# Distances and residual rows in one group of products, and the first block's edges and next messages ahead of its inverse

## The chip, the cores and the metric

The kernel runs on one core of a Trainium2 chip. The metric is the device time of one execution in microseconds; the kernel before was measured three times, and one more execution was taken by the hardware profiler. Five engines work side by side, each through its own queue in order: TensorE (PE, matrix products; its weight loads are shown as PEld), VectorE (DVE), ScalarE (ACT), GpSimd (POOL) and SyncE (SP, which here only issues DMAs). Products land in PSUM, which has eight banks of 512 float32 per partition; VectorE and ScalarE read them out.

## The reference

Two graph layers on 128 graphs of 128 nodes with 256 features, all in float32. The change lies in layer 0, where h is the rectified layer norm of x:

```python
h  = relu(bn(conv1d(xc, conv1_w)))             # 1 tap
h  = bn(conv1d(h, conv2_w, pad 8))             # 17 taps
x_conv = relu(h + xc)
s  = x @ w_se.T + b_se                         # 3 numbers a node
sq = sum(s * s)
dist = sq[:, :, None] + sq[:, None, :] - 2 * s @ s.T
A    = exp(-dist) * mask
msg  = relu(x @ w_msg.T + b_msg)
x_nmp = A @ msg
gi = concat(x_conv, x_nmp) @ w_ih.T + b_ih ;  gh = x @ w_hh.T + b_hh
r, z = sigmoid(gi_r + gh_r), sigmoid(gi_z + gh_z)
out  = (1 - z) * tanh(gi_n + r * gh_n) + z * x
```

Layer 1 takes the first 25 nodes of each graph, in five groups of nodes, through two normalised graph convolutions and adds the result.

## The kernel before

The graphs are taken in 32 blocks of four (`BB` = 4, `NBLK` = 32). The 17-tap convolution is done in the frequency domain in an earlier part of the kernel; its result lies in DRAM as 128 main rows (`yd`) and 8 residual rows (`yrd`) per graph. The part that the change touches runs from about 449 us to the end and is a loop over blocks: `gates(i)` makes block i's gates while, in between its products, the inputs of block i + 1 are made.

What is made for a block, in functions of these names:

- `messages`: seven products (L544, 130 columns: 128 of the messages and the 3 of s, by a scheme with seven products for eight), evicted by VectorE, ScalarE and GpSimd into `msg`; then VectorE writes s and its squares into the small tile `lr` (L570 to L575).
- `conv_out`, the inverse transform: into four banks, first the residual rows (L519: four products that are 16 rows deep, each on another fourth of the array's rows, left open), then the main rows (L523: two products a bank, which close it). VectorE (L526) and ScalarE (L527) make `xc` of it.
- `edge_terms`: two transposes of `lr` (L582), which ScalarE copies to `lt` (L584).
- `edges`: four products 5 rows deep (L594, the distances; again on different fourths of the array), each in a bank of its own; ScalarE takes the exponential (L597), VectorE multiplies with the mask (L599).
- `x_nmp`: eight products (L609), copied to `xn` by ScalarE (L614) and VectorE (L612).
- `gate_inputs`: sums of blocks of the three inputs (L632 to L635), on GpSimd for `xc` and `ht`, on VectorE for `xn`.

`gates` goes through four units of seven products each, in the order 1, 2, 6, 5, 3, 7, 4 (z: 1, 6, 5, 7, 4, 2, 3). They are r (three matmuls a product: `ht`, `xc`, `xn`), nh (one: `ht`), nn (two: `xc`, `xn`) and z (three). All are L658. Each product takes a bank and is evicted in turn: product 1 by ScalarE (m1, L661), 2 by VectorE (L663), 6 by VectorE (u2, L666), 5 by ScalarE (m5, L669), which lets GpSimd make u4 = u2 + m5 (L671); 3 is added to u4 by VectorE (L673), 7 gives u3 on VectorE (L676), from which GpSimd makes the last quarter (L677), and 4 is subtracted by VectorE (L679). After the r unit, ScalarE applies two sigmoids (L694); after nn, two tanh (L704). The hook of the z unit runs what is left of the next block's inputs.

After each product `step()` is called: every other time it goes on by one `yield` in `beside_gates(i + 1)`, which calls the functions above, and otherwise in layer 1. So the order of the yields in `beside_gates` is the order of the work on TensorE. `beside_gates` also takes block i - 1 through `back` (its output, and the layer-1 preparation, with the transposes L822 and the product L835). Layer 1's own products are L926, L986 and L905; they stand between block 12's and 14's, between 22's and 24's, and at the end. For block 0 there are no gates to work beside: `sums_ahead` is called after each product of block 0's nh unit, which is taken first there, and makes block 0's inputs at fixed places of that unit.

Banks come from one pool of eight (`bank()`). Which bank a product gets, and so which eviction it waits for, is settled when the program is built.

Of the kernel before, what the change touches and what calls it, by code (L numbers as in the profile page):

```python
# [17 lines left out]
BB = 4  # L18
# [8 lines left out]
MW = 130  # L27
# [47 lines left out]
def gnn_kernel(ctx: ExitStack, tc: tile.TileContext, io, out0: bass.AP, out1: bass.AP):  # L75
    nc = tc.nc
    x, adjT = io["x"], io["adjT"]
    NBLK, N, _, D = x.shape
# [288 lines left out]
    v = {}  # L367
# [138 lines left out]

    A_s, xcs, xns, ts, msgs, outs, lrs, xts = ({} for _ in range(8))

    def conv_out(i):

        ht = hts[i]
        ym, yr = loaded.pop(i)
        xc = wk.tile([P, C, T], F32, tag="xc", name="xc", bufs=2)
        pss = [[bank()[:, :H] for _ in range(2)] for _ in range(C)]
        for o in range(C):
            for h, ps in enumerate(pss[o]):
                r0 = 32 * (2 * o + h)
                g = slice(r0, r0 + 2 * NR)
                nc.tensor.matmul(ps, yr[g, :], idr[g, :], start=True, stop=False)  # L519
        for o in range(C):  # L520
            for h, ps in enumerate(pss[o]):
                for b in range(2):
                    nc.tensor.matmul(ps[:, b * N:(b + 1) * N], ym[:, 2 * h + b, o * P:(o + 1) * P], idm,  # L523
                                     start=False, stop=b == 1)
                v = slice(h * H, (h + 1) * H)
                nc.vector.scalar_tensor_tensor(xc[:, o, v], ps, sc2[:, o:o + 1], ht[:, o, v], op0=ALU.mult, op1=ALU.add)  # L526
            nc.scalar.activation(xc[:, o, :], xc[:, o, :], AF.Relu, bias=sh2[:, o:o + 1])  # L527
            yield
        xcs[i] = xc

    def messages(i):


        msg = wk.tile([P, BB, 2, MW], F32, tag="msg", name="msg", bufs=1)
        b11, b12, b21, b22 = quarters(hts[i])
        t1, t2, t3, t4 = (ts[i][2][:, m] for m in range(4))
        s2, s3, s4 = (swm[:, m] for m in range(3))
        ops = ((wms[:, 0, 0], b11), (wms[:, 1, 0], b21), (s4, b22), (wms[:, 1, 1], t4), (wms[:, 0, 1], t1), (s2, t2), (s3, t3))

# [35 lines left out]
        nc.vector.tensor_scalar(lr[:, 0, :, 4:5], lr[:, 1, :, 3:4], -1.0, None, op0=ALU.mult)  # L575
        yield

    def edge_terms(i):

        ps = bank()  # L580
        for k in range(2):
            nc.tensor.transpose(ps[:, k * P:(k + 1) * P], lr[:, k].rearrange("p b r -> p (b r)"), ident)  # L582
        lt = wk.tile([P, 2, P], F32, tag="lt", name="lt", bufs=2)
        nc.scalar.copy(lt.rearrange("p k n -> p (k n)"), ps[:, :2 * P])  # L584
        lrs[i] = lt

    def edges(i):

        at = ats.pop(i)
        lt = lrs.pop(i)  # L590
        pd = [bank() for _ in range(BB)]
        for b in range(BB):
            g = slice(32 * b, 32 * b + 5)
            nc.tensor.matmul(pd[b][:, :N], lt[g, 0, :], lt[g, 1, :], start=True, stop=True)  # L594
        e = wk.tile([P, BB, N], F32, tag="e", name="e", bufs=1)
        for b in range(BB):
            nc.scalar.activation(e[:, b, :], pd[b][:, :N], AF.Exp)  # L597
            if b % 2:
                nc.vector.tensor_mul(e[:, b - 1:b + 1, :], e[:, b - 1:b + 1, :], at[:, b - 1:b + 1, :])  # L599
        A_s[i] = e  # L600

    def x_nmp(i):

# [399 lines left out]
    def beside_gates(i):  # L1003

        ends = back(i - 2, *back_loads(i - 2)) if i > 1 else iter(())
        if i < NBLK:
            parts = messages(i)
            next(parts)
            yield
            next(parts)  # L1010
            next(ends, None)
            yield
            yield
            inverse = conv_out(i) if i else iter(())
            next(inverse, None)
            next(ends, None)
            yield
            edge_terms(i)
            next(ends, None)
            yield  # L1020
            for _ in inverse:
                yield
            edges(i)
            yield
            next(ends, None)
            yield
            yield
            yield from x_nmp(i)
        for _ in ends:
            yield  # L1030
            if i == NBLK:
                yield
# [12 lines left out]
    load_y(0)  # L1045
    load_y(1)
    degs = degrees(*degree_loads())
    begin = beside_gates(0)
    for _ in range(2):
        next(begin)  # L1050
    held = [7]

    def sums_ahead():

        held[0] -= 1
        if held[0] == 3:
            for _ in conv_out(0):
                pass
            gate_inputs(0, (0,))
            while 0 not in lrs:  # L1060
                next(begin)
        if held[0] == 2:
            while 0 not in A_s:
                next(begin)
        if held[0] == 0:
            for _ in begin:
                pass
            gate_inputs(0, (1,))
            gate_inputs(1, (2,))

    layer1s = []
    for i in range(NBLK):
        first = beside_gates(i + 1)
        turn = [0]

        def step():

            next(degs, None)
            turn[0] += 1
            if (turn[0] % 2 if i else turn[0] % 3) and next(first, STOP) is not STOP:  # L1080
                return
            for _ in range(2 if i == NBLK - 1 else 1):
                while layer1s and next(layer1s[0], STOP) is STOP:
                    layer1s.pop(0)

        if i + 2 < NBLK:
            load_h(i + 2)
            load_y(i + 2)
        xts[i] = wk.tile([P, C, T], F32, tag="xt", name="xt", bufs=2)
        nc.sync.dma_start(xts[i], io["xT"][i])  # L1090

        def nxt():
            for _ in first:
                pass
            if i + 1 < NBLK:
                gate_inputs(i + 1, (0, 1))
            if i + 2 < NBLK:
                gate_inputs(i + 2, (2,))

        gates(i, step, nxt, None if i else sums_ahead)  # L1100
        if (i + 2) * BB == PARTS[0]:
            for q in (-5, -4, -3):
                prepare(q)
        for k in range(len(PARTS)):
            if i * BB == first_of[k + 1]:
                layer1s.append(layer1(k))
# [136 lines left out]
```

## Time and profile before

| | |
|---|---|
| median of three executions | 1865.76 us (1865.35 to 1867.79) |
| profiled execution, its own time | 1866.29 us |
| span of the profiled execution | 1864.5 us, mean granted TensorE clock 0.997 |
| TensorE busy | 1843.8 us, 99% of the span |
| VectorE busy | 1361.9 us, 73% |
| ScalarE busy | 737.0 us, 40% |
| GpSimd busy | 652.9 us, 35% |
| distances, L594: 256 records | 16.1 us busy |
| residual rows, L519: 256 records | 24.6 us busy |

The span is the time from the first instruction's start to the last one's end. A float32 product is two records on TensorE, one per pass. Matmuls overlap in the pipeline, so a record (380 ns for 256 columns) is longer than the step from one to the next (216 ns); steps are read from the starts. The idle time behind an engine's row, in square brackets in a timeline, is followed by what ended it. The "granted clock" is the share of its full speed at which TensorE was allowed to run.

### The profile page before, as it was taken

The page shows a single profiled execution, that of the slowest core. Times are in us where ns is not written, and L with a number is a line of the kernel's source. Part 1 is how long each engine was busy: PE and PEld are TensorE (multiplying, and loading weights), DVE is VectorE, ACT ScalarE, POOL GpSimd, SP SyncE. Part 2 cuts the span into 40 slices and gives each one's busy share as a digit, 9 for nine tenths or more (in the row PEclk, how much of TensorE's full clock was granted, in tenths as well). Part 3 has the DMA queues.
Part 4 walks back from the last instruction along what each step waited for, and adds up shares of the span by engine and source line. Part 5 has one row for each costly group of instructions (what it writes and reads, how often), then busy time and mean ns, then how long its engine had stood idle before and what let it go on. Part 6 is the DMA issues. An engine that isn't in the chain of part 4 may idle for free.

```text
span 1864.5 us, 31417 instructions
## 1 busy us (share of the span) xinstructions
PE 1843.8 (99%) x10982; PEld 1592.3 (85%) x10982; DVE 1361.9 (73%) x3312; ACT 737.0 (40%) x1668; POOL 652.9 (35%) x803
## 2 busy tenths in 40 slices
PE   8999999999999999999999999999999999999998
PEld 6888888887888888888888888888888888888887
DVE  6888865555988888888656778888756788888643
ACT  4666651111443334333334433433343343334334
POOL 1111125675343544454321345444412243544200
PEclk9999999999999999999999999999999999999999
DMA  8788778997532233224234422333232433222125
GB/s 294 285 303 334 302 277 285 344 325 244 171 88 75 72 85 94 76 73 124 73 90 119 120 75 72 88 83 113 61 103 85 131 95 87 73 72 70 39 89 158
DMA packets 219420, 267.98 MB, mean 144 GB/s; under 512 B 106210, under 2 KB 182967, under 8 KB 217215
## 3 DMA queue, kind: packets, MB, share of 16 engines
q1 hardware_dynamic: 214079, 248.04, 42.8%
q10 hardware_dynamic: 5184, 17.93, 2.4%
q8 instruction: 88, 1.44, 0.3%
q14 instruction: 69, 0.57, 0.1%
HBM read 169.24 MB, written 96.67 MB: 143 GB/s over the span
## 4 chain that ended last, share of the span: by engine, by line
PE 90%; DVE 4%; DMA 2%; POOL 2%; SPq 1%; issue 1%; ACT 1%; ACTq 0%; DVEq 0%; POOLq 0%
PE bank L658 43%; PE bank L332 6%; PE bank L235 6%; PE bank L926 5%; PE bank L986 5%; PE bank L544 4%; PE bank L251 4%; PE bank L523 3%; PE bank L327 3%; PE bank L609 3%; PE bank L172 2%; PE bank L221 1%; PE bank L905 1%; DMA nt<-in_adjN_dram 1%; PE bank L835 1%; PE bank L519 1%
## 5 line engine op out<-in xcount | busy, mean ns | idle before, releaser
L658 PE MATMUL bank<-t,sw 128*128 128x256 f32 x1152 | 291.4, 380 | 0.0
L671 POOL TENSOR_TENSOR u<-u,m 128x256 f32<-128x256 f32 x128 | 93.7, 732 | 465.1 <-ACT m L669 386.7
L658 PEld LDWEIGHTS bank<-t,sw 128*128 128x128 f32 x1152 | 212.7, 190 | 29.0 <-issue 2.3
L658 PE MATMUL bank<-t,wih 128*128 128x256 f32 x768 | 197.2, 379 | 0.0
L658 PEld LDWEIGHTS bank<-t,wih 128*128 128x128 f32 x768 | 145.5, 190 | 20.9 <-issue 0.9
L235 PE MATMUL bank<-wc,ht 128*128 128x256 f32 x512 | 126.0, 390 | 0.0
L324 POOL TENSOR_TENSOR vs<-v 128x256 f32<-128x256 f32 x134 | 99.0, 763 | 70.9 <-DMA v<-vd 44.1
L658 PE MATMUL bank<-t,whh 128*128 128x256 f32 x384 | 117.5, 388 | 0.0
L567 ACT ACTIVATE msg<-msg 128x512 f32<-128x512 f32 x64 | 36.9, 622 | 196.7 <-DVE msg L563 196.7
L658 PE MATMUL bank<-xc,wih 128*128 128x256 f32 x384 | 114.4, 379 | 0.0
L658 PE MATMUL bank<-xn,wih 128*128 128x256 f32 x384 | 114.2, 379 | 0.0
L986 PE MATMUL bank<-w,hh 128*125 128x256 f32 (+9 forms) x480 | 113.5, 380 | 0.6 <-DVE hh L931 0.6
L658 PE MATMUL bank<-ht,whh 128*128 128x256 f32 x384 | 109.9, 380 | 0.0
L205 POOL TENSOR_TENSOR rs<-ve,mhalf 128x4 f32<-128x4 f32 x32 | 32.3, 1009 | 217.0 <-DVE ve L203 209.9
L926 PE MATMUL bank<-ax,w 128*128 128x500 f32 (+8 forms) x416 | 107.0, 396 | 0.1
L235 PEld LDWEIGHTS bank<-wc,ht 128*128 128x128 f32 x512 | 93.8, 193 | 15.1 <-issue 0.3
L986 PEld LDWEIGHTS bank<-w,hh 128*125 128x125 f32 (+9 forms) x480 | 84.3, 178 | 18.8 <-DVE hh L931 1.0
L180 ACT COPY sp<-bank 128x272 f32<-128x272 f32 x208 | 67.0, 408 | 68.7 <-PE bank L172 52.9
L676 DVE TENSOR_TENSOR u<-bank,u 128x256 f32<-128x256 f32 x128 | 53.7, 420 | 54.6 <-PE bank L658 53.0
L321 DVE SCALAR_TENSOR_TENSOR s<-X 128x256 f32<-128x256 f32 x67 | 45.0, 672 | 64.9 <-PE bank L332 64.9
L669 ACT COPY m<-bank 128x256 f32<-128x256 f32 x128 | 47.3, 369 | 104.5 <-PE bank L658 104.5
L926 PEld LDWEIGHTS bank<-ax,w 128*128 128x128 f32 x416 | 69.9, 190 | 19.4 <-issue 12.3
(206 smaller groups left out, 4415.8 us busy)
## 6 DMA issues: line engine op xcount, KB each, us to landing
vd<-sp SPq DMA_DIRECT2D x16, 2176.0 KB
v<-vd SPq DMA_DIRECT2D x34, 1024.0 KB
w<-in_w_dram SPq DMA_DIRECT2D x40, 512.0 KB
ln<-in_x_dram SPq DMA_DIRECT2D x32, 512.0 KB
htd<-ht SPq DMA_DIRECT2D x32, 512.0 KB
yd<-ys ACTq DMA_DIRECT2D x32, 512.0 KB
ht<-htd SPq DMA_DIRECT2D x32, 512.0 KB
ym<-yd SPq DMA_DIRECT2D x32, 512.0 KB
```

What stands on the lines that cost most here:

```text
L180: nc.scalar.copy(dst, s)
L235: nc.tensor.matmul(pv[:, bb, :], ht[:, c, b * N:(b + 1) * N], wc1[:, c, :], start=c == 0, stop=c == C - 1)
L251: nc.tensor.matmul(ps[:, bb * LW:(bb + 1) * LW], h1[:, 2 * h + bb, c * P:(c + 1) * P], fd, start=True, stop=True)
L324: nc.gpsimd.tensor_tensor(vs[:, c], vr[c], vi[c], op=ALU.add)
L327: nc.tensor.matmul(p1[:, :D], a[:, c], vs[:, c], start=c == 0, stop=c == C - 1)
L332: nc.tensor.matmul(ps[:, k * D:(k + 1) * D], u[:, c], w[c], start=c == 0, stop=c == C - 1)
L523: nc.tensor.matmul(ps[:, b * N:(b + 1) * N], ym[:, 2 * h + b, o * P:(o + 1) * P], idm, start=False, stop=b == 1)
L544: nc.tensor.matmul(ps[:, b, :], d[:, b * N:(b + 1) * N], w, start=True, stop=True)
L658: nc.tensor.matmul(ps, w, d, start=n == 0, stop=n == len(pairs) - 1)
L671: nc.gpsimd.tensor_tensor(got["u4"], got["u2"], got["m5"], op=ALU.add)
L926: nc.tensor.matmul(pv[:, q - q0, :], w1s[k5 + g][:, c, q * P:(q + 1) * P], xv[:, c], start=c == 0, stop=c == C - 1)
L986: nc.tensor.matmul(ps[:n1, :D], hh[:, q, at:at + n1], w2s[k5 + g][:, q, :], start=q == 0, stop=q == HID // P - 1)
```

## The change

From the second block on, the four distances are computed in the same banks as the residual rows, in columns 256 to 383 beside the inverse's columns 0 to 255, and right before them: eight thin products in one group instead of two groups of four. `edges` and `conv_out` are split accordingly into `residual_rows` (distances, residual rows, and by `exponentials` the exponential and the mask) and a `conv_out` that starts with the main rows. In `beside_gates` the transposes of `lr` move ahead to where the inverse began; the group follows two yields later, then the main rows, then x_nmp. The whole has one yield more.

Block 0 keeps its distances apart (`edges`), but the order is changed: transposes and distances first, at other places of the nh unit; then the first four message products of block 1; then residual rows and inverse; then x_nmp. `gate_inputs(1, (2,))`, which those messages need, is called earlier, and the message tile `msg` has two buffers instead of one.

```diff
+    def residual_rows(i):
+
+        yr = loaded[i][1]
+        pss = [[bank() for _ in range(2)] for _ in range(C)]
+        if i:
+            lt = lrs.pop(i)
+            for b in range(BB):
+                g = slice(32 * b, 32 * b + 5)
+                nc.tensor.matmul(pss[b // 2][b % 2][:, H:H + N], lt[g, 0, :], lt[g, 1, :], start=True, stop=True)
         for o in range(C):
             for h, ps in enumerate(pss[o]):
                 r0 = 32 * (2 * o + h)
                 g = slice(r0, r0 + 2 * NR)
-                nc.tensor.matmul(ps, yr[g, :], idr[g, :], start=True, stop=False)
+                nc.tensor.matmul(ps[:, :H], yr[g, :], idr[g, :], start=True, stop=False)
+        if i:
+            exponentials(i, [pss[b // 2][b % 2][:, H:H + N] for b in range(BB)])
+        return pss
...
-        msg = wk.tile([P, BB, 2, MW], F32, tag="msg", name="msg", bufs=1)
+        msg = wk.tile([P, BB, 2, MW], F32, tag="msg", name="msg", bufs=2)
...
-    def edges(i):
+    def exponentials(i, pd):
 
         at = ats.pop(i)
-        lt = lrs.pop(i)
-        pd = [bank() for _ in range(BB)]
-        for b in range(BB):
-            g = slice(32 * b, 32 * b + 5)
-            nc.tensor.matmul(pd[b][:, :N], lt[g, 0, :], lt[g, 1, :], start=True, stop=True)
         e = wk.tile([P, BB, N], F32, tag="e", name="e", bufs=1)
         for b in range(BB):
-            nc.scalar.activation(e[:, b, :], pd[b][:, :N], AF.Exp)
+            nc.scalar.activation(e[:, b, :], pd[b], AF.Exp)
             if b % 2:
                 nc.vector.tensor_mul(e[:, b - 1:b + 1, :], e[:, b - 1:b + 1, :], at[:, b - 1:b + 1, :])
         A_s[i] = e
+
+    def edges(i):
+
+        lt = lrs.pop(i)
+        pd = [bank()[:, :N] for _ in range(BB)]
+        for b in range(BB):
+            g = slice(32 * b, 32 * b + 5)
+            nc.tensor.matmul(pd[b], lt[g, 0, :], lt[g, 1, :], start=True, stop=True)
+        exponentials(i, pd)
...
             yield
-            inverse = conv_out(i) if i else iter(())
-            next(inverse, None)
-            next(ends, None)
-            yield
             edge_terms(i)
             next(ends, None)
             yield
+            yield
+            if i:
+                inverse = conv_out(i, residual_rows(i))
+            else:
+                edges(i)
+                inverse = iter(())
+            yield
+            next(ends, None)
+            yield
             for _ in inverse:
                 yield
-            edges(i)
-            yield
             next(ends, None)
-            yield
             yield
             yield from x_nmp(i)
...
-    begin = beside_gates(0)
+    begin, second = beside_gates(0), beside_gates(1)
     for _ in range(2):
         next(begin)
+    gate_inputs(1, (2,))
     held = [7]
 
     def sums_ahead():
 
         held[0] -= 1
         if held[0] == 3:
-            for _ in conv_out(0):
-                pass
-            gate_inputs(0, (0,))
             while 0 not in lrs:
                 next(begin)
-        if held[0] == 2:
+        if held[0] == 1:
             while 0 not in A_s:
                 next(begin)
         if held[0] == 0:
+            next(second)
+            for _ in conv_out(0, residual_rows(0)):
+                pass
+            gate_inputs(0, (0,))
             for _ in begin:
                 pass
             gate_inputs(0, (1,))
-            gate_inputs(1, (2,))
...
-        first = beside_gates(i + 1)
+        first = beside_gates(i + 1) if i else second
```

More of the change, by code (lines that the diff above doesn't have):

```diff
@@ L507, in gnn_kernel @@
     A_s, xcs, xns, ts, msgs, outs, lrs, xts = ({} for _ in range(8))
[L509 to L514, printed above, removed]
+    def residual_rows(i):
[6 more added lines that the diff above has]
+                nc.tensor.matmul(pss[b // 2][b % 2][:, H:H + N], lt[g, 0, :], lt[g, 1, :], start=True, stop=True)
         for o in range(C):
@@ L518, in conv_out @@
                 g = slice(r0, r0 + 2 * NR)
-                nc.tensor.matmul(ps, yr[g, :], idr[g, :], start=True, stop=False)
+                nc.tensor.matmul(ps[:, :H], yr[g, :], idr[g, :], start=True, stop=False)
+        if i:
+            exponentials(i, [pss[b // 2][b % 2][:, H:H + N] for b in range(BB)])
+        return pss
+    def conv_out(i, pss):
+        ht = hts[i]
+        ym = loaded.pop(i)[0]
+        xc = wk.tile([P, C, T], F32, tag="xc", name="xc", bufs=2)
         for o in range(C):
@@ L525, in conv_out @@
                 v = slice(h * H, (h + 1) * H)
-                nc.vector.scalar_tensor_tensor(xc[:, o, v], ps, sc2[:, o:o + 1], ht[:, o, v], op0=ALU.mult, op1=ALU.add)
+                nc.vector.scalar_tensor_tensor(xc[:, o, v], ps[:, :H], sc2[:, o:o + 1], ht[:, o, v], op0=ALU.mult, op1=ALU.add)
             nc.scalar.activation(xc[:, o, :], xc[:, o, :], AF.Relu, bias=sh2[:, o:o + 1])
@@ L1013, in beside_gates @@
             yield
-            inverse = conv_out(i) if i else iter(())
-            next(inverse, None)
+            edge_terms(i)
             next(ends, None)
             yield
-            edge_terms(i)
+            yield
[5 more added lines that the diff above has]
+            yield
             next(ends, None)
```

## The prediction

> **What bounds the kernel now.** I read the page first (busy time by engine), then TensorE's waits, then the timelines of the engines through one ordinary block. The page:
>
> ```profile
> PE 1843.8 (99%) x10982; PEld 1592.3 (85%) x10982; DVE 1361.9 (73%) x3312; ACT 737.0 (40%) x1668; POOL 652.9 (35%) x803
> ```
>
> TensorE (PE) is busy for all but 20.7 us of the 1864.5 us span. A change can gain only by taking work from TensorE, or a few us of waits; it can lose wherever it makes TensorE wait. The two waits near this change:
>
> ```profile
> PE bank L519 <- DMA yr<-yrd: 3.2, 1, 3.2
> PE bank L609 <- DVE e L599: 0.4, 2, 0.2
> ```
>
> Both are in block 0. Now block 5, TensorE's timeline (start, length, line, operands, count of records; a 128x256 product is two records, 0.433 us):
>
> ```profile
> 622.06 1.03 PE L658 MATMUL bank<-t,wih 128*128 128x256 f32 x4
> 623.02 0.71 PE L519 MATMUL bank<-idr,yr 16*128 16x256 f32 x8
> 623.66 1.16 PE L523 MATMUL bank<-idm,ym 128*128 128x128 f32 x8
> 624.66 1.03 PE L658 MATMUL bank<-ht,whh 128*128 128x256 f32 x4
> 625.52 0.38 PE L582 MATMUL bank<-ident,lr 128*128 128x128 f32 x2
> 625.74 0.38 PE L822 MATMUL bank<-ident,xl 128*100 128x128 f32 x2
> ...
> 626.82 1.05 PE L523 MATMUL bank<-idm,ym 128*128 128x128 f32 x8
> 627.72 0.60 PE L658 MATMUL bank<-ht,sw 128*128 128x256 f32 x2
> 628.15 0.59 PE L658 MATMUL bank<-t,sw 128*128 128x256 f32 x2
> 628.67 0.50 PE L594 MATMUL bank<-lt 5*128 5x128 f32 x8
> 629.11 0.70 PE L658 MATMUL bank<-t,whh 128*128 128x256 f32 x2
> 629.64 0.59 PE L658 MATMUL bank<-xc,wih 128*128 128x256 f32 x2
> ```
>
> Each thin group (16 or 5 rows deep, four products side by side in the array) has a way in, a body and a way out. Residual rows, L519: the products before end at 622.06 + 4 x 0.2165 = 622.93 and the group starts at 623.02 (in: 0.09); body 0.64 to 623.66; the eight records after it take 1.00, where the same eight at 626.82 take 0.90 (out: 0.10). Distances, L594: 628.15 + 0.43 = 628.58, start 628.67 (0.09); body 0.44; the next product takes 0.53 for 0.43 (0.10). So 0.83 and 0.63 us.
>
> The other engines at the same time; first ScalarE, then VectorE and GpSimd:
>
> ```profile
> 622.71 0.35 ACT L669 COPY m<-bank 128x256 f32<-128x256 f32 x1
> 624.36 0.72 ACT L694 ACTIVATE o<-o,brz 128x512 f32<-128x512 f32 x1 [1.29 <-DVE o L673]
> 625.50 0.72 ACT L694 ACTIVATE o<-o,brz 128x512 f32<-128x512 f32 x1 [0.43 <-POOL o L677]
> 626.13 0.35 ACT L661 COPY m<-bank 128x256 f32<-128x256 f32 x1
> 626.39 0.72 ACT L527 ACTIVATE xc<-xc,bn 128x512 f32<-128x512 f32 x1
> 627.01 0.36 ACT L584 COPY lt<-bank 128x256 f32<-128x256 f32 x1
> ```
>
> ```profile
> 622.61 0.17 DVE L575 TENSOR_SCALAR lr<-lr 128x4 f32<-128x4 f32 x1
> 626.52 0.42 DVE L663 TENSOR_TENSOR nh<-bank,m 128x256 f32<-128x256 f32 x1 [0.55 <-ACT m L661]
> 627.20 0.41 DVE L666 TENSOR_TENSOR u<-bank,m 128x256 f32<-128x256 f32 x1
> ```
>
> ```profile
> 623.14 0.72 POOL L671 TENSOR_TENSOR u<-u,m 128x256 f32<-128x256 f32 x1 [3.18 <-ACT m L669]
> ```
>
> What to see: the evictions run far behind TensorE. `lr` is complete at 622.78, and nh's first copy (L661) runs at 626.13, behind the second sigmoid. TensorE doesn't wait, because its banks are free in time.
>
> **The change, ordinary block.** 26 blocks have this pattern (2 to 12, 15 to 22, 25 to 31); those that follow one another start 36.53 us apart (block 5: 612.03 to 648.55). Removed: one way in and one way out, 0.09 + 0.10 = 0.19 us. The merged body isn't in the trace: between 0.98 (0.10 less, if one weight load hides under the products before it) and 1.27 (the two groups unmerged); I take 0.44 + 0.64 = 1.08. Without waits that is -0.19 us a block.
>
> Now the order, with the times of block 5. TensorE comes to the transposes of `lr` where the residual rows stood: 622.93. `lr` is there at 622.78, so no wait (at most 0.1). Transposes 0.22, four nh products 4 x 0.433 = 1.73, way in 0.09: ready for the distances at 624.97.
>
> First new wait. The distances need the copy of the transposes to `lt`, and ScalarE's queue in the changed kernel is: copy of r's product 5 (old L669), first sigmoid (L694), `lt`, second sigmoid, nh's copies, table load, exponentials. The first sigmoid starts at 624.36, held by VectorE's L673, itself held by the GpSimd row at 623.14, the same rows as before. The instruction behind such an activation starts 0.62 later (626.39 to 627.01), so `lt` runs 624.98 to 625.34, and the distances start at 625.40 instead of 624.97: 0.43 us. Queued behind: all of TensorE.
>
> Second new wait. From the distances until VectorE has read the inverse, four of the eight banks are held, across nine gate matmuls and the layer-1 transposes; all else turns in the other four. nn's first product gets the bank of nh's product 3, so it waits until VectorE's add (L673) has read that. The chain: second sigmoid 625.50; nh's copy m1 626.13 to 626.48 (`lt` fits in the gap before, so nothing shifts); VectorE's add 626.52; u2 at the next slot, 626.86 to 627.27 (the statistics that stood there come later now); GpSimd's sum 0.06 later, 0.73 long: 628.06; VectorE's L673 0.05 later, 0.41 long: 628.52; TensorE about 0.05 after: 628.57. TensorE itself would be there at 625.40 + 1.08 + 0.10 + two products 0.87 + transposes 0.22 + one product 0.43 = 628.10. Wait 0.47. As this chain doesn't start from TensorE's place, it sets the moment whatever the merged group costs: with the first wait gone the second would be 0.90.
>
> From nn's first product to the next block it was 648.55 - 629.64 = 18.91; both halves of the inverse (0.90 each) now come after it: 20.71. So the next block starts at 628.57 + 20.71 = 649.28, not 648.55: **+0.73 us a block**. Nothing gives it back: from z's fourth product on, VectorE works without a pause up to `lr`, and that product stays as far ahead of the next block as before, so each block repeats the wait.
>
> Moved and covered: the exponentials (table load 1.28, four in 0.79) end near 628.9, and the inverse that waits for them in its banks starts at 629.4; its cover is nn's first product (0.87), and without it they'd cost up to 0.4. The mask's multiply ends near 629.3, long before x_nmp (637). x_nmp ends 18 products (7.8 us) ahead of the next block instead of 24; its readers are VectorE's four sums, which had been waiting 2.1 + 0.87 us there. SP's loads stay in order.
>
> Here the Trainium skill speaks against the change: "TensorEngine Tiling (Array Packing)", section "Restrictions and Gotchas", warns that row tiling raises the pressure on PSUM because each row tile takes its own bank. Its "Key Properties" say that a change of tiling mode drains the array, which the 0.09 and 0.10 agree with. By the drain rule alone the sum is -0.19 a block; the pressure rule has no price, and the rows above give it one.
>
> **Other blocks.** In 10, 12, 15, 22 and 25 m1's copy ends 3.83 after the place of the residual rows instead of 3.45: 0.37 more. In the four blocks amid layer 1 (13, 14, 23, 24) 1.7 us of layer-1 products stand between the steps; I take -0.19 each (bounds -0.3 and +0.9, the ordinary block with the later chain).
>
> Start: block 0 has two thin groups for three (-0.8), and no wait for `yr`. But TensorE now comes first to block 0's transposes, and its `lr` is written by VectorE at 457.05, where the wait for `yr` had ended at 457.18: 3.1 us takes the place of 3.2. The granted clock was 0.50 from 457.20 to 463.40 after that idle, and stays so. The two 0.2 us waits for e go (-0.4); block 1's transposes come after nine matmuls (3.9 us) where its chain to `lr` took 3.9 beside less work, and it now starts later behind x_nmp's sums: +1.2 (bounds 0 and 3). With block 1's -0.2 the start is -0.2, bounds -2 and +3. Message tiles in two buffers cost nothing; they let block 1's messages begin early.
>
> Sum: 26 x 0.73 = 19.0; 5 x 0.37 = 1.9; 4 x -0.19 = -0.8; start -0.2: +19.9. The profiled execution took 1866.29 (1.8 around its span), so 1886.2; the median shown is 0.5 lower: **1885.7 us**, 1.1% slower.
>
> **Rivals.**
> - No waits: a bank comes free before TensorE needs it. 31 x -0.19 = -5.9, start -0.2: 1860. For it: TensorE hardly waits now. Against: the chain from the sigmoid to 628.57 is measured row by row. It decides if that chain ends 0.9 us earlier. Chance 0.09.
> - Only the first wait: 26 x (0.43 - 0.19) = 6, others -1: 1871. For it: the second is 0.47 on top. Against: the bank is assigned, not chosen at run time. 0.12.
> - VectorE falls behind too: what it has to do after x_nmp no longer fits, z's reads come late, and each block loses about 0.5 more: 26 x 0.5 = 13: 1899. Against: some 1.8 us of slack by the same sums. 0.12.
> - The merging does nothing (1.27 for 1.08): pinned as above, so the forecast's time; counted in it.
>
> **How the numbers follow.** Forecast 0.67, with 0.2 a block either way: 1880 to 1891. Only the first rival and the far halves of the other two are left out: the range is 1870 to 1899. A measurement tells 0.2% (3.7 us) from no change. Faster is the first rival, 0.09; "same" is the edge between it and the second, 0.04; slower the rest.
>
> **What would show it.** Right: waits of TensorE at the distances on ScalarE's `lt`, some 0.4 x 26, and at nn's first product on VectorE's nh, some 0.5 x 26; blocks 37.26 apart; the wait for `yr` gone and one on `lr` in its place; one thin group a block. Wrong: blocks 36.3 apart (no waits), 36.8 (the first alone), or VectorE pausing nowhere before z.

## The result, and the profile after

The changed kernel takes 1889.98 us (median of four executions, 1889.56 to 1893.35) where the kernel before took 1866.74 us beside it: a ratio of 1.0129, 95% interval 1.0111 to 1.0146. It is 1.1% to 1.5% slower. The forecast was 1885.7 us, the range 1870 to 1899. Two single executions in the experiments below took more than twice the usual time (4144 and 4754 us), and the ranges given there leave them out. The profiled execution of after took 1889.56 us, its span 1887.7 us at a granted clock of 0.995.

The page, busy time by engine and then the chain that ended last, by engine:

```profile
PE 1843.8 (98%) x10982; PEld 1588.0 (84%) x10982; DVE 1325.6 (70%) x3312; ACT 736.1 (39%) x1667; POOL 677.4 (36%) x803
PE 69%; DVE 19%; POOL 3%; issue 2%; ACT 2%; DMA 2%; SPq 1%; DVEq 0%; ACTq 0%; POOLq 0%
```

TensorE (PE) has as many records and as much busy time as before, to a tenth of a microsecond, and a span 23.2 us longer. In the chain that ended last VectorE (DVE) has 19%, where it had 4%, and TensorE 69%, where it had 90%. So the time went into waits of TensorE. These are its waits from the loop over blocks that count here (total, times, longest):

```profile
PE bank L517 <- ACT lt L596: 7.2, 21, 0.4
PE bank L674 <- DVE nh L689: 6.7, 22, 0.3
PE bank L674 <- ACT m L677: 4.2, 21, 0.2
PE bank L556 <- DVE m L566: 4.0, 3, 1.7
...
PE bank L594 <- DVE lr L587: 3.2, 1, 3.2
```

The first three come some 21 times each, once an ordinary block: the first at the distances (L517), the second at nn's first product, the third at nh's product 3. The fourth comes three times, at the messages (L556). The last, once, is the wait on `lr` that stands where the wait for `yr` was. Block 5 of after, 611.37 to 648.77, in the timeline of TensorE (start, length, engine, line, operands, number of records; in brackets the idle time before, and what ended it):

```profile
622.27 0.38 PE L594 MATMUL bank<-ident,lr 128*128 128x128 f32 x2
...
624.71 0.50 PE L517 MATMUL bank<-lt 5*128 5x128 f32 x8 [0.34 <-ACT lt L596]
625.04 0.61 PE L522 MATMUL bank<-idr,yr 16*128 16x256 f32 x8
625.86 0.70 PE L674 MATMUL bank<-ht,sw 128*128 128x256 f32 x2 [0.20 <-ACT m L677]
...
627.97 0.70 PE L674 MATMUL bank<-xc,wih 128*128 128x256 f32 x2 [0.30 <-DVE nh L689]
```

The three waits are 0.34 + 0.20 + 0.30 = 0.84 us. Block 6 begins 37.40 us after block 5, where it was 36.53. A record's length reaches past the start of the next (0.59 for two records that follow one another 0.43 apart), so each bracket is some 0.15 short of what the wait costs; this, too, hides in TensorE's busy time. With 0.15 added to each, the three make 1.29 us; an ordinary block is 1.28 us longer than one without a wait (36.12, below). What TensorE waits for, in the order in which it happens; first ScalarE, then GpSimd, then VectorE:

```profile
620.98 1.15 ACT L579 ACTIVATE msg<-msg 128x512 f32<-128x512 f32 x2 [7.06 <-DVE msg L575]
622.04 0.35 ACT L685 COPY m<-bank 128x256 f32<-128x256 f32 x1
623.68 0.72 ACT L710 ACTIVATE o<-o,brz 128x512 f32<-128x512 f32 x1 [1.29 <-DVE o L689]
624.31 0.35 ACT L596 COPY lt<-bank 128x256 f32<-128x256 f32 x1
624.82 0.72 ACT L710 ACTIVATE o<-o,brz 128x512 f32<-128x512 f32 x1 [0.16 <-POOL o L693]
625.45 0.35 ACT L677 COPY m<-bank 128x256 f32<-128x256 f32 x1
```

```profile
622.47 0.72 POOL L687 TENSOR_TENSOR u<-u,m 128x256 f32<-128x256 f32 x1 [3.18 <-ACT m L685]
```

```profile
623.22 0.42 DVE L689 TENSOR_TENSOR o<-bank,u 128x256 f32<-128x256 f32 x1 [1.12 <-POOL u L687]
...
627.49 0.42 DVE L689 TENSOR_TENSOR nh<-bank,u 128x256 f32<-128x256 f32 x1 [0.90 <-POOL u L687]
```

Read from the top: ScalarE makes the two Relus of the messages (L579, 1.15 us), and behind them stands the copy of r's product 5 (L685), done at 622.39. GpSimd's sum waited 3.18 us for that copy alone. From it VectorE makes `o` (623.22), from that ScalarE the first sigmoid (623.68), and behind the first sigmoid stands `lt` (624.31), which lets the distances go at 624.71. Behind the second sigmoid stands m1 (625.45), which lets nh's product 3 go at 625.86; through u2 and GpSimd's sum comes VectorE's nh at 627.49, which lets nn go at 627.97.

Where the 23.2 us came from, by stage. Every row is the difference of two starts of first message products in the timeline, so "block" here is the stretch from one block's first messages to the next one's:

| stage | before | after | difference |
|---|---|---|---|
| all ahead of block 0 | 448.98 | 448.16 | -0.82 |
| blocks 0 and 1 | 53.47 | 51.66 | -1.81 |
| 2 to 9 | 292.21 | 298.53 | +6.32 |
| 10 and 11 | 73.73 | 78.29 | +4.56 |
| 12 to 14 (layer 1) | 179.21 | 181.52 | +2.31 |
| 15 to 21 | 256.00 | 260.53 | +4.53 |
| 22 to 24 (layer 1) | 178.65 | 181.50 | +2.85 |
| 25 to 30 | 219.47 | 223.13 | +3.66 |
| 31 to the end | 162.77 | 164.40 | +1.63 |
| span | 1864.50 | 1887.73 | +23.23 |

Two things in this table weren't forecast. First, blocks 15 and 25 take 36.12 where they took 36.84 before: they have no wait at all. That is 0.41 less than the 36.53 of an ordinary block before; whether merging gives it is for the experiments to tell. Second, block 10 alone takes 40.89 for 37.20. Block 15 in TensorE's timeline of after:

```profile
1071.10 0.50 PE L517 MATMUL bank<-lt 5*128 5x128 f32 x8
1071.43 0.61 PE L522 MATMUL bank<-idr,yr 16*128 16x256 f32 x8
1071.97 0.70 PE L674 MATMUL bank<-ht,sw 128*128 128x256 f32 x2
```

From the first distance to the next gate product it is 0.33 + 0.54 = 0.87 us.

### The profile page after: what moved, and what is told of

Same layout as the page of the kernel before. It is cut to its first block, busy times and chain, and to the rows that moved or that the text cites. A ratio compares the mean times of both kernels' runs of the same rounds, so it can differ in the third digit from the quotient of the medians.

```text
span 1887.7 us, 31328 instructions
## 1 busy us (share of the span) xinstructions
PE 1843.8 (98%) x10982; PEld 1588.0 (84%) x10982; DVE 1325.6 (70%) x3312; ACT 736.1 (39%) x1667; POOL 677.4 (36%) x803
## 3 DMA queue, kind: packets, MB, share of 16 engines
q8 instruction: 87, 1.43, 0.3%
## 4 chain that ended last, share of the span: by engine, by line
PE 69%; DVE 19%; POOL 3%; issue 2%; ACT 2%; DMA 2%; SPq 1%; DVEq 0%; ACTq 0%; POOLq 0%
PE bank L674 27%; PE bank L332 6%; PE bank L235 6%; PE bank L1002 5%; PE bank L942 5%; PE bank L251 3%; PE bank L327 3%; PE bank L535 3%; DVE o L728 3%; DVE xt L815 3%; PE bank L625 3%; PE bank L172 2%; POOL u L687 2%; PE bank L556 2%; DMA nt<-in_adjN_dram 1%
## 5 line engine op out<-in xcount | busy, mean ns | idle before, releaser
L579 ACT ACTIVATE msg<-msg 128x512 f32<-128x512 f32 x64 | 36.9, 622 | 195.0 <-DVE msg L575 194.9
L692 DVE TENSOR_TENSOR u<-bank,u 128x256 f32<-128x256 f32 x128 | 53.5, 418 | 58.0 <-PE bank L674 57.6
L685 ACT COPY m<-bank 128x256 f32<-128x256 f32 x128 | 47.0, 367 | 108.5 <-PE bank L674 108.5
L674 PEld LDWEIGHTS bank<-xc,wih 128*128 128x128 f32 x384 | 68.5, 190 | 23.2 <-DVE nh L689 15.7
```

What stands on the lines that cost most here:

```text
L674: nc.tensor.matmul(ps, w, d, start=n == 0, stop=n == len(pairs) - 1)
```

## The experiments

The theory after the comparison had three parts. (a) In ordinary blocks one chain, from the copy of r's product 5 through sigmoids and sums to nh, sets when nn may begin. (b) Merging in itself saves 0.41 us a block. (c) In blocks 10, 12 and 22 VectorE is late for another reason. The rivals stand with each experiment. The planner spoken of in them is the part of the language that orders each engine's instructions when the program is built; `keep_in_program_order` ties an instruction behind the one written before it on its engine.

### `lt` ahead of the first sigmoid

```
-            nc.scalar.activation(r[:, q, :], r[:, q, :], AF.Sigmoid, bias=brz[:, q:q + 1])
+            s = nc.scalar.activation(r[:, q, :], r[:, q, :], AF.Sigmoid, bias=brz[:, q:q + 1])
+            if q == 0 and not ahead:
+                tc.keep_in_program_order(s)
```

The copy to `lt` is written ahead of the sigmoids, but the planner had put the first sigmoid ahead of it; the edit keeps the order as written.

> Only ScalarE's order differs from the changed kernel: the copy to lt stands ahead of the first sigmoid, in the time in which ScalarE idles (block 5 of the changed kernel: from 622.39 to 623.68), so lt should be there about 1.3 us before TensorE comes to the distances, and the wait there (0.34 a block, 7.2 in all) goes. Theory (the chain from r's product 5 through the sigmoids to nh's sums sets when nn may begin, whatever stands before it): the waits at nh's product 3 and at nn's first product grow from 0.20 and 0.31 to 0.85 together, ordinary blocks stay 37.40 apart, time 1888 to 1891. Rival (the waits add up): 0.34 less in each of some 22 blocks, 37.06 apart, time about 1882.

Measured: 1892.74 us (1891.89 to 1892.90), ratio to before 1.0138 (1.0116 to 1.0160). Blocks are 37.40 apart. TensorE's two largest waits:

```profile
PE bank L674 <- ACT m L677: 7.8, 21, 0.4
PE bank L674 <- DVE nh L689: 7.3, 22, 0.3
```

The wait on `lt` is gone from the list, all 7.2 us of it, and the distance between blocks (the period) is the same to 0.01: the wait at nh's product 3 grew from 0.20 to 0.37 each, the one at nn's first product from 0.30 to 0.33. The theory holds, the rival (0.34 less a block) falls. Its profiled span is 3.3 us longer than that of the changed kernel; 2.6 of this lie ahead of block 0, whose messages start at 450.77 for 448.16, and 0.8 from block 31 on. The code ahead of block 0 is the same; over the twelve profiles of this case that start lies between 447.4 and 452.2 us.

### The Relus of the messages behind the exponentials

```
-        for b in range(0, BB, 2):
-            nc.scalar.activation(mf[:, b:b + 2, :D], mf[:, b:b + 2, :D], AF.Relu)
         msgs[i] = mf
...
         A_s[i] = e
+        mf = msgs[i]
+        for b in range(0, BB, 2):
+            tc.keep_in_program_order(nc.scalar.activation(mf[:, b:b + 2, :D], mf[:, b:b + 2, :D], AF.Relu))
```

> The two Relus of the messages (1.15 us on ScalarE, between VectorE's last message and the copy of r's product 5) are put behind the exponentials; nothing else moves. Theory: this copy is the head of the chain that pins nn, GpSimd's sum waits for it alone, so the chain from there to nn's first product comes about 1.06 us earlier, at 626.9 where TensorE would be at 626.8 in block 5: all three waits go but for about 0.1, ordinary blocks 36.2 apart instead of 37.40, blocks 15 and 25 unchanged at 36.12, block 10's waits on VectorE unchanged; time about 1863 (1858 to 1868). Rival (the waits come from the banks that the open group holds, or from VectorE being behind, and ScalarE's Relus have slack): 37.3 to 37.4 apart, time 1888 to 1891.

Measured: 1863.32 us (1862.27 to 1864.25), ratio 0.9981 (0.9972 to 0.9991). Blocks are 36.20 apart; 15 and 25 take 36.12, block 10 40.80. In block 5 (609.02 to 645.22), TensorE and then ScalarE:

```profile
621.96 0.50 PE L517 MATMUL bank<-lt 5*128 5x128 f32 x8
622.28 0.61 PE L522 MATMUL bank<-idr,yr 16*128 16x256 f32 x8
622.83 0.70 PE L675 MATMUL bank<-ht,sw 128*128 128x256 f32 x2
...
624.45 0.67 PE L675 MATMUL bank<-xc,wih 128*128 128x256 f32 x2
624.95 0.59 PE L675 MATMUL bank<-xn,wih 128*128 128x256 f32 x2
```

```profile
620.12 0.72 ACT L711 ACTIVATE o<-o,brz 128x512 f32<-128x512 f32 x1 [3.46 <-DVE o L690]
620.75 0.35 ACT L594 COPY lt<-bank 128x256 f32<-128x256 f32 x1
...
624.48 1.17 ACT L608 ACTIVATE msg<-msg 128x512 f32<-128x512 f32 x2
```

No bracket is left on TensorE; only nn's first two records take 0.50 (624.45 to 624.95) where they take 0.43 in block 15. The Relus run at 624.48, in time that ScalarE had free, and all else on the chain comes earlier: the first sigmoid starts 11.10 us after the block's start, where it was 12.31. Moving 1.15 us of work on an engine that is busy 39% of the time took 1.20 us out of each ordinary block. This shows (a): the head of the chain was on ScalarE's queue. The rival, that the banks held by the open group make TensorE wait whatever the evictions do, falls; the same products stand between the group and the inverse here.

### The same edit on the kernel before

The edit is the one above, made on the kernel before.

> The kernel before with the two Relus of the messages behind the exponentials, nothing else. Theory: its evictions run late too, but its banks are free in time, so a shorter chain shortens nothing: blocks 36.53 apart, time 1866 to 1867.5, ratio 1.000. Rival (ScalarE's Relus cost time in any order, and the gain of this edit on the changed kernel has nothing to do with the new order): some tenths less a block, 1855 to 1862.

Measured: 1865.89 us (11 executions), ratio 0.9987 (0.9979 to 0.9996); ordinary blocks are 36.53 apart, as before; block 10 is 0.67 shorter. So the Relus cost next to nothing in the old order, where TensorE comes to the distances and to nn only when the late copies are done. The price belongs to the new order and the Relus together.

### The merged group taken apart at its place

Distances and residual rows are made by two functions, with one step (nh's products 3 and 7) and the layer-1 transposes between them:

```
-                inverse = conv_out(i, residual_rows(i))
+                pss = distances(i)
...
             yield
             next(ends, None)
+            if i:
+                inverse = conv_out(i, residual_rows(i, pss))
             yield
```

> The merged group is taken apart again at the same place and in the same banks: the four distances, then nh's products 3 and 7 and the transposes of the layer-1 step, then the four residual rows. Theory: one more way in and way out and the overlap lost, 0.41 to 0.47, which shows in full where nothing waits (blocks 15 and 25: 36.12 to about 36.55), but for the most part hides in the wait for the pinned chain in ordinary blocks (37.40 to about 37.65); time about 1896 (1893 to 1899). Rival (waits add to whatever TensorE has to do): ordinary blocks 37.85, time about 1903. If merging were worth nothing: 36.12 in blocks 15 and 25 and 37.40 elsewhere, 1890.

Measured: 1905.21 us (1903.15 to 1907.34), ratio 1.0208 (1.0190 to 1.0225). Ordinary blocks are 37.67 apart, blocks 15 and 25 take 36.53. Both are what the theory gave, to 0.02: 0.41 more where nothing waits, 0.27 more where the chain hides a part. The time is 6 us above the theory's interval. That lies in stages for which it had no number: block 2 waits like the others here (37.67 for 36.72), block 6 takes 39.31, and from block 10 to 14, 22 to 24 and from 31 on it is 2.6, 1.4 and 1.9 us above after. What holds these up wasn't tried.

### Both together

> Both edits together on the changed kernel: the Relus behind the exponentials, and the merged group taken apart at its place, so the price of merging can be read where nothing waits. Theory (merging saves one way in, one way out and the overlap of the weight loads, 0.41 as blocks 15 and 25 show): ordinary blocks 36.20 + 0.41 = 36.61 apart, so that merging alone turns 36.61 into 36.20 and the new order without merging is worth nothing against 36.53; time about 1876 (1873 to 1880). Rival (only a way in and a way out are saved, 0.19): 36.39 apart, about 1869.

Measured: 1877.92 us (1876.86 to 1882.79), ratio 1.0057 (1.0044 to 1.0070). Ordinary blocks are 36.53 apart, 15 and 25 take 36.53 as well. So with no wait and no merging the new order has exactly the period of the old one, 36.53, and merging takes it to 36.12 (blocks 15 and 25; 0.08 of wait is left in the 36.20 of the others, which is why the 36.61 was too high). Beside 36.53, 36.39 (a way in and a way out only) is excluded. That the time is still 0.6% above the kernel before comes from blocks 10, 12 to 14 and 22 to 24, which are 10.4 us longer together; they are taken up below. In block 15 of the kernel that is split but has the Relus where they were (the section above), in TensorE's timeline, the two bodies are apart:

```profile
1078.38 0.50 PE L515 MATMUL bank<-lt 5*128 5x128 f32 x8
1078.81 0.70 PE L678 MATMUL bank<-ht,sw 128*128 128x256 f32 x2
...
1080.09 0.71 PE L526 MATMUL bank<-idr,yr 16*128 16x256 f32 x8
1080.73 0.70 PE L678 MATMUL bank<-t,whh 128*128 128x256 f32 x2
```

0.43 + 0.64 = 1.07 apart, 0.87 merged: 0.20 of overlap beside the 0.19 for a way in and a way out. Where the overlap lies is seen in TensorE's weight loads (PEld), in block 15 of the changed kernel:

```profile
1071.10 0.31 PEld L517 LDWEIGHTS bank<-lt 5*128 5x128 f32 x8 [0.33 <-ACT m L677]
1071.32 0.32 PEld L522 LDWEIGHTS bank<-idr,yr 16*128 16x128 f32 x8
```

The loads for the residual rows begin 0.22 after those for the distances, whose products are recorded until 1071.60: the two groups overlap. From the first load for the residual rows to the next gate product (1071.97) it is 0.65, as much as the 0.64 apart.

### The merged group one step later

```
             edge_terms(i)
             next(ends, None)
             yield
             yield
+            yield
             if i:
                 inverse = conv_out(i, residual_rows(i))
...
-            yield
             next(ends, None)
             yield
+            yield
             for _ in inverse:
                 yield
             next(ends, None)
-            yield
             yield from x_nmp(i)
```

> The merged group and the inverse come one step (two of nh's products) later than in the changed kernel; x_nmp stays. Theory: the wait on lt goes, as TensorE comes to the distances after 625.1 in block 5 and lt is there at 624.7; but the group's third and fourth bank are now those of nh's products 1 and 2, which the late chain frees only at 625.8 and 626.3, so about 1.1 us of wait stands at the distances, on VectorE's nh, and nn's first product still waits for nh's third sum: blocks stay near 37.4 apart, time 1886 to 1893. Rival (the order was the fault: the group held four banks too early, and later all waits go): 36.1 to 36.3 apart, time about 1858.

Measured: 1907.47 us (1906.41 to 1909.20), ratio 1.0220 (1.0205 to 1.0236); blocks 38.27 apart. Neither the theory nor the rival gave that. In block 5 (617.58 to 655.87), TensorE, and then VectorE:

```profile
631.38 0.49 PE L517 MATMUL bank<-lt 5*128 5x128 f32 x4
632.09 0.83 PE L517 MATMUL bank<-lt 5*128 5x128 f32 x3 [0.21 <-ACT m L677]
...
633.40 0.42 PE L838 MATMUL bank<-ident,xl 128*100 128x128 f32 x2
...
636.79 1.13 PE L674 MATMUL bank<-t,sw 128*128 128x256 f32 x4 [0.59 <-DVE mv L843]
```

```profile
635.40 0.94 DVE L606 TENSOR_TENSOR e<-e,at 128x256 f32<-128x256 f32 x2
636.27 0.17 DVE L842 BATCH_NORM_AGGREGATE mv<-st 100x2 f32<-100x6 f32 x1
636.36 0.38 DVE L695 TENSOR_TENSOR nh<-u,bank 128x256 f32<-128x256 f32 x1
```

The wait at the group's later banks is there as the theory had it: from the first distance to what follows the group it is 2.02 us instead of 0.87, 1.15 more where 1.1 was expected. But another, at nn, is new: nn's product 6 takes the bank of nh's product 4, and VectorE reads that (L695) only at 636.36, behind the layer-1 statistic and the mask, which the planner had put ahead of it. (The bracket names the row behind L695, which ends 0.06 later; in block 6 it names L695.) So the run doesn't tell theory and rival apart. It shows only that this later place, with the other engines' order as it is, is no gain.

### The start alone

The kernel before with the new `sums_ahead`, the messages of block 1 ahead and two buffers for them; the rest is as before.

> The kernel before with the new order of block 0 alone (first messages of block 1 ahead of block 0's inverse, the edges ahead of it, two buffers for the messages). Theory: the part up to block 2 is worth what the two traces show, 2.63 us, less the 0.4 that the merged group of block 1 saves there: time about 1864.5, blocks from 2 on 36.53 apart. Rival (the gain at the start came from the merged group or is lost again at the end): 1866 to 1867.

Measured: 1865.94 us (12 executions, 1864.10 to 1870.97), ratio 0.9994 (0.9984 to 1.0003): the time can't tell it from nothing. The stage of blocks 0 and 1 takes 52.04 for 53.47, a gain of 1.43; with the merged group of block 1 (0.41) that makes about the 1.81 of the table. The other 0.8 that the start seemed to gain are within the spread of the part ahead of it. Blocks 10 to 14 take 1.7 us more here, so all of the gain is gone by block 15, as the rival had it, though not at the end; why these blocks lose by the new start isn't shown.

### Where blocks 10, 12 and 22 lose

These blocks' messages wait for VectorE, and VectorE is late since the block before. VectorE in the stretch that leads to block 12, in the profile of before (block 12 starts at 868.39) and of after (876.65):

```profile
860.06 0.68 DVE L612 COPY xn<-bank 128x512 f32<-128x512 f32 x1
862.54 0.29 DVE L863 TENSOR_TENSOR nt<-nt,ident 125x125 f32<-125x125 f32 x1 [1.79 <-DMA nt<-in_adjN_dram]
...
865.19 0.42 DVE L679 TENSOR_TENSOR z<-u,bank 128x256 f32<-128x256 f32 x1
```

```profile
869.08 0.69 DVE L628 COPY xn<-bank 128x512 f32<-128x512 f32 x1 [0.40 <-PE bank L625]
874.41 0.29 DVE L879 TENSOR_TENSOR nt<-nt,ident 125x125 f32<-125x125 f32 x1 [4.65 <-DMA nt<-in_adjN_dram]
...
875.59 0.42 DVE L692 TENSOR_TENSOR u<-bank,u 128x256 f32<-128x256 f32 x1
...
876.94 0.41 DVE L695 TENSOR_TENSOR z<-u,bank 128x256 f32<-128x256 f32 x1
```

VectorE stands 4.65 us for the load of `nt`, a layer-1 matrix that isn't needed yet, and z's sum, which the gates do need, comes 0.29 after the start of block 12 where it came 3.20 ahead of it. (The Trainium skill, "PSUM — Partial Sum Buffer", section "Engine vs sequencer instructions", calls the queues of ScalarE, VectorE and GpSimd strictly first in, first out; these rows agree: u's sum (L692) came only behind those on `nt`, at 875.59, though TensorE had finished the product that it reads by 871.63.) Why `nt` is late shows in SP's queue, here ahead of block 10, before (794.66) and after (798.36):

```profile
779.32 4.09 SPq L845 DMA_DIRECT2D xa<-ab  x5
783.46 1.28 SPq L856 DMA_DIRECT2D nt<-in_adjN_dram  x3
```

```profile
786.10 4.15 SPq L861 DMA_DIRECT2D xa<-ab  x5
790.30 1.28 SPq L872 DMA_DIRECT2D nt<-in_adjN_dram  x3
```

The loads of `nt` stand behind the stores of the layer-1 step, and these wait for that step's last product (old L835, new L851). It stands behind both halves of the inverse and came later with them: 18.48 us into block 9 before (776.61), 22.81 after (783.76). From 11.20 us ahead of the block the loads came to 8.06 ahead.

That the stores make the loads late is read from these rows; no run issued the loads apart from the stores. Three runs take VectorE's two operations on `nt` ("sums" below) back to their place in the program, beside layer 1; the second of them was tied to the first already. The three are: with the late Relus, on the kernel before, and on the changed kernel alone.

```
-            ops = [nc.vector.tensor_add(nt[:n, :n], nt[:n, :n], ident[:n, :n]),
+            ops = [tc.keep_in_program_order(nc.vector.tensor_add(nt[:n, :n], nt[:n, :n], ident[:n, :n])),
                    nc.vector.tensor_mul(nt[:n, :n], nt[:n, :n], dc[:n, :n])]
```

> On top of the late Relus: VectorE's two sums on the layer-1 matrices nt, which the planner had moved ahead into blocks 9, 11, 21 and 31, are kept in the order of the program, beside layer 1. Theory: in those blocks VectorE stood 2.6 to 4.65 us for the loads of nt, which SP issues behind the stores of the layer-1 step that the change moved back, and its lag is what the messages of blocks 10, 12 and 22 wait for (3.7, 1.4 and 0.9 us more than before). With the sums elsewhere block 10 comes down from 40.8 to about 36.9, 12 and 22 by about 1 each; time about 1858 (1855 to 1862). Rival (VectorE is behind there for another reason, or the stall only moves into the blocks with layer 1): 1862 to 1865.

> The kernel before with VectorE's sums on nt kept in the order of the program, nothing else. Theory (the loads of nt came about 3 us later by the change, and only then did VectorE's wait for them reach the messages): before, VectorE stood only 1.1 to 2.5 us and TensorE waited 0.3 in each of blocks 10, 12 and 22, so the edit is worth about 0.7 in block 10, 0.4 around 12 and 22, 1 to 3 us in all: 1864 to 1867. Rival (the sums were badly placed in any order and the change has no part in it): 9 to 12 us here too, about 1857.

> The changed kernel with the same edit alone, the Relus where they were. Theory (three causes that add up: the chain in ordinary blocks, VectorE's wait for nt ahead of blocks 10, 12, 22 and 31, and against them the merging): ordinary blocks unchanged at 37.40, block 10 from 40.89 to 37.4, blocks 12 to 14 and 22 to 24 about 2 to 3 shorter each, time about 1880 (1877 to 1883). Rival (with the chain late, the messages of these blocks wait anyway): 1886 to 1890.

Measured, by stage, in us ("sums" is this edit, "Relus" the late Relus):

| stage | before | before + sums | after | after + sums | after + Relus | after + Relus + sums |
|---|---|---|---|---|---|---|
| blocks 0 and 1 | 53.47 | 53.54 | 51.66 | 51.47 | 51.75 | 51.56 |
| 2 to 9 | 292.21 | 292.21 | 298.53 | 298.55 | 289.50 | 289.51 |
| 10 and 11 | 73.73 | 73.05 | 78.29 | 74.81 | 77.01 | 72.39 |
| 12 to 14 | 179.21 | 178.19 | 181.52 | 178.64 | 180.35 | 177.41 |
| 15 to 21 | 256.00 | 256.02 | 260.53 | 260.56 | 253.36 | 253.28 |
| 22 to 24 | 178.65 | 177.81 | 181.50 | 178.02 | 179.89 | 176.86 |
| 25 to 30 | 219.47 | 219.48 | 223.13 | 223.16 | 217.11 | 217.10 |
| 31 to the end | 162.77 | 161.57 | 164.40 | 165.48 | 163.72 | 162.67 |
| median, us | 1866.7 to 1868.0 | 1862.21 | 1889.98 | 1881.70 | 1863.32 | 1850.55 |
| ratio to before | | 0.9971 | 1.0129 | 1.0070 | 0.9981 | 0.9904 |
| 95% interval | | 0.9960 to 0.9982 | 1.0111 to 1.0146 | 1.0053 to 1.0087 | 0.9972 to 0.9991 | 0.9892 to 0.9917 |

On the changed kernel the edit takes 9.84 us out of blocks 10 to 14 and 22 to 24 (3.48 + 2.88 + 3.48) and nothing out of ordinary blocks; on the kernel before it takes 2.54 there. So some 7.3 us of what these stretches lost came from the sums that stood waiting for the later loads. From block 31 on the edit works the other way: 1.20 less on the kernel before, 1.08 more on the changed one. Over the whole loop the difference is therefore some 5 us, and why the end behaves so isn't known.

On the changed kernel alone the theory is right (1881.70 in 1877 to 1883, ordinary blocks unchanged), and the causes nearly add up. For the kernel before it was too low: the kernel gains 0.2% to 0.4%, some 5 us, more than the 1 to 3 forecast and less than the rival's 9 to 12. The sums stood badly there too, and the change made it worse. With both edits the time (1850.55) lies 4 us below the theory's interval (1855 to 1862): block 10 fell to 36.20 and not to 36.9, and the stretches 12 to 14 and 22 to 24 by 3 us each and not by 1. No wait on messages is left then. TensorE's longest wait beyond the spectral part is:

```profile
PE bank L592 <- DVE lr L585: 3.5, 2, 3.2
```

This last version, the changed kernel with late Relus and tied sums, takes 1850.55 us (1850.50 to 1850.67), 0.8% to 1.1% below the kernel before and below all others here. Not all of that belongs to the change: beside the kernel before with tied sums it is 11.7 us less. The kernel before with both edits wasn't run.

## Why the prediction was right

Point by point, by its steps:

- **The first new wait was right**: the distances on ScalarE's `lt`, 0.34 us of idle time (0.49 with the 0.15 that a bracket is short) for 0.43, 21 times. But the run with `lt` ahead shows that it decided nothing.
- **The second new wait, and that its chain sets the moment, was right.** nn's first product was forecast 16.54 us after the block's start; it stands at 16.60. The wait itself is split: 0.20 is already spent at nh's product 3, whose bank waits for m1 on the same chain (the working had TensorE arrive there just in time; as the merged body is 0.21 shorter than was taken, it comes too early), and 0.30 is left at nn. The run with `lt` ahead is the forecast's own sentence, "with the first wait gone the second would be 0.90", in numbers: 0.37 + 0.33 of idle time, each some 0.15 short, with the period unchanged.
- **The period** was forecast at 37.26 and is 37.40: 0.06 is in nn's start, 0.09 in the stretch behind it. The 19 blocks of 3 to 9, 11, 16 to 21, 26 to 30 give 16.5 us of the 23.2.
- **The merged body was mis-sized**: 1.08 taken (bounds 0.98 to 1.27), 0.87 measured, outside the bounds. Merging saves 0.41 where nothing waits, not 0.19. It cost the forecast nothing in ordinary blocks, since the chain sets the moment there, which is also why the gain doesn't appear. "Key Properties" of the Trainium skill's "TensorEngine Tiling (Array Packing)" says, beside the drain that the forecast weighed, that different tiles can load weights and multiply in parallel; the 0.20 of overlap agrees with that. The warning of pressure on PSUM, from the same page, bears on the case only together with the late evictions: TensorE waited for banks, but with the evictions earlier these waits went, and no run changed the number of banks.
- **"0.37 more" in blocks 10, 12, 15, 22 and 25 failed.** In 15 and 25 there is no wait: the copy of r's product 5 ends at 1066.50, 2.56 us ahead of the transposes (1069.06), where in block 5 it ends 0.12 after them. So -0.72 each stands for the +1.10 forecast. Block 10, with the sums tied in both kernels, takes 37.39 for 36.53: +0.86, as an ordinary block, with no 0.37 on top.
- **"SP's loads stay in order" was the step that failed in blocks 10, 12 and 22.** The loads of `nt` did stay behind the same stores. The time didn't: the last product of the layer-1 step came later with the inverse, so its stores did, and the loads behind them. The forecast's third rival, VectorE falling behind, is what happened here, though in three blocks, through a load, and not in every block. It cost some 7.3 us in the stretches 10 to 14 and 22 to 24, by the tied sums.
- **The start** gained 1.81 for the 0.2 forecast (whose own terms add up to 0.3). The wait on `lr` took the place of the one on `yr`, 3.2 for 3.2, as forecast; the 1.2 us of waiting at block 1's transposes didn't come.
- **The blocks amid layer 1**, once the sums are tied in both kernels, differ by +0.45 (12 to 14) and +0.21 (22 to 24); the forecast had +0.73 + 0.37 - 0.38 = +0.72 for each of these stretches.

So the mechanism of the ordinary block was right, and the time came out within 5 us in part by luck, as errors of the other terms cancelled. 1.6 at the start and 3.6 in blocks 15 and 25 were forecast too high, and smaller terms too (block 2, which takes 36.72, by 0.5). 2.7 in the ordinary blocks (19 x 0.14) were too low, and the loads, some 7.3, weren't forecast at all. What stays open is the end: from block 31 on after takes 1.63 us more, of which 0.87 is the ordinary block; over the runs this stage lies between 161.6 and 166.3.

## What to carry to other kernels

When work of the engine that bounds is moved ahead, follow the eviction chain of the new neighbours back to its head, and look at what stands in that queue ahead of the head and isn't needed yet: 1.15 us of Relus on an engine 39% busy made the difference between a gain of 0.3 us a block (36.20 for 36.53) and a loss of 0.9 (37.40). Removing a single wait on that chain gained nothing; the head had to come earlier. And a step that is moved takes with it whatever the DMA queue has behind its stores, and an engine that takes its work in order, as VectorE did here, passes the lateness of a load on to work that has nothing to do with it.

## What was not expected of the hardware

Two groups of row-tiled products with different depths (5 and 16 rows), one behind the other, overlap: 0.87 us for bodies that take 0.43 and 0.64 apart. The time up to block 0, some 450 us of the same code, differs between the twelve profiles by up to 4.7 us (447.4 to 452.2), which is as large as several effects of this case; only the stages, not the single times, could tell those apart.
